# Turning a graph's adjacency as packed bytes on VectorE instead of as bf16 on TensorE

## The chip, the cores and the metric

The kernel runs on one core of a Trainium2 chip. The metric is the device time of one execution in microseconds (us), lower is better. Engines are named as in the profile: PE is TensorE (PEld its weight loads), DVE is VectorE, ACT is ScalarE, POOL is GpSimd, SP is SyncE, which here only issues DMAs. Each engine works through its own instructions in order; between engines they wait for each other by semaphores.

## The reference

64 graphs of 256 nodes with 512 features go through two pre-norm attention layers whose attention is masked by the graph's adjacency. Layer 0 has 4 heads of 64, layer 1 has 8. Cut to what matters:

```python
h = relu(layernorm(x))
q, k, v = heads(h @ Wq), heads(h @ Wk), heads(h @ Wv)
sim = einsum('bhid,bhjd->bhij', q, k) * scale
sim = where(adjacency_mask[:, None], sim, -max)      # layer 1: graph_mask | eye, else -1e9
x = x + einsum('bhij,bhjd->bhid', softmax(sim), v) @ Wo + bo
```

`adj` comes as one byte per entry (0 or 1), 256 x 256 for each graph. In layer 0 a row without any neighbour becomes a uniform softmax; layer 1 always has the diagonal.

## The kernel before

**Steps.** Two graphs make one step, so there are 32 steps (`NSTEP`), and T = 512 tokens in a step, kept as four tiles of 128 rows. Three steps are in work at once: while layer 1 of step s runs, layer 0 of step s+1 is finished and layer 0 of step s+2 is begun. One such period takes 95.67 us in the middle of the run.

**Order.** Nothing is scheduled automatically on PE, DVE, ACT and POOL. `at(period, place, fn, ...)` writes an event with a place; the events are sorted by place and the instructions of each engine stand in that order. A period is 6.4 places long. Within it PE has: 0.0 to 1.0 the first q and k of layer 1 (line 817); 1.0 the output combination of layer 1 of the step before (line 914, 28 instructions, seen as 56 records); 2.0 a visit (weighing by probabilities, line 1041, then new scores, line 970) and the values of layer 1 (line 898); 3.0 the combination of layer 0 of step s+1 (line 914, 14 instructions, 28 records); 3.5 the second q and k of layer 1 (817); 4.5 a visit and q, k of layer 0 of step s+2 (817); 5.5 the values of layer 0 (864); 6.2 a third visit.

**Products.** Every large matrix product is done as 7 block products (Winograd's scheme), numbered 1 to 7. Each fills a PSUM bank, and an "evacuation" (`evacuate`, `accumulate`, lines 746 to 785) takes the bank out and adds it into its place, on DVE for most products and on ACT for products 1 and 2. There are four banks in rotation (`mm_tile`), and a bank can be written again only when its evacuation is done. Three products go into a bank that another has used, on top of what stands in it (`SHARED = {2: 1, 4: 7, 3: 5}`): product 4 is accumulated in product 7's bank, so it may start only after product 7 has been evacuated. The tuples `SET`, `SETC` and `SETC0` are the orders in which the seven are done; `SETC0` is that of layer 0's combination, (1, 6, 5, 2, 7, 3, 4). After some products POOL adds a common term `u` to a block of `xt` (line 785).

**The adjacency.** The scores are computed with the keys on the partitions, so the adjacency has to be turned. For a step: `load_adjacency` (line 488) brings the bytes by SP's queue at place 1.0 of the period before; `adjacency_cast` (513, POOL, place 0.45) makes bf16 of them; `adjacency_turn` (563, place 2.5, in the midst of layer 1's values) turns eight 128 x 128 blocks on PE into a bank, and ACT copies the bank to `adT` (568). `mask0` (574, 577, POOL, place 3.1) makes layer 0's mask (adT - 1) * 1e30 and multiplies it by the row's "has neighbours" flag `ne`; `mask1` (582, 585, place 5.85) makes layer 1's. `adb` and `adT` share one buffer (tag "ab"). `neighbours` (521, DVE) reduces the bytes to the flags.

**Other work near it.** On DVE the sums over keys are turned and reduced (`turn_keys`, `key_quarters`, lines 1011 and 1018; `turn_sums`, `key_sums`, lines 1071 to 1083); DVE also turns h in 32 x 32 blocks (`turn_blocks`, 700), which SP moves by DMA (712). On POOL stand the sums of the probabilities' halves (`key_halves`, 1005), the division by the sums (`normalise`, 1116), the block sums for the products (`act_sums0`, `act_sums1`, 405 to 410) and the biases (`first_bias` 508, `second_bias` 652). `first_bias` for the four token tiles, in the order 2, 3, 0, 1, is at places 2.34, 2.5, 2.85, 2.86.

Of the kernel before, what the change touches and what calls it, by code (L numbers as in the profile page):

```python
# [8 lines left out]
FP = mybir.dt.float32  # L9
BF = mybir.dt.bfloat16  # L10
U8 = mybir.dt.uint8
I32 = mybir.dt.int32
AF = mybir.ActivationFunctionType
ALU = mybir.AluOpType

EPS = 1e-5
BIG = 1e30
# [298 lines left out]
def fast_path(  # L316
# [19 lines left out]
    nc = tc.nc  # L336
    P = 128
    B, N, D = x.shape
    DH = 64
    G = 2  # L340
    NSTEP = B // G
    NIC = N // P
    NT = G * NIC
# [9 lines left out]
    act = ctx.enter_context(tc.tile_pool(name="act", bufs=1))  # L353
# [10 lines left out]
    def mm_tile(shape, dt=FP, hold=False):  # L364
        tag = next(b for b in banks if b not in held)
        banks.remove(tag)
        banks.append(tag)
        if hold:
            held.add(tag)
        return ps_mm.tile(shape, dt, name="mm", tag=tag)  # L370

    identb = const.tile([P, P], BF, name="identb")
# [16 lines left out]

    NB = 7
    A_OF = {(0, 0): 0, (0, 1): 1, (1, 0): 2, (1, 1): 3}
    B_OF = ((0, 6, 5), (1, 3, 1))
    PRODUCT = {1: (0, 0), 2: (1, 1), 3: (6, 2), 4: (3, 6), 5: (2, 3), 6: (4, 4), 7: (5, 5)}
# [78 lines left out]
    S = [dict() for _ in range(NSTEP)]  # L474
# [10 lines left out]

    def load_adjacency(s):
        ad = S[s]["ad"] = io.tile([P, NT, N], U8, name="ad", bufs=1)
        nc.sync.dma_start(ad, adj[s * G:(s + 1) * G].rearrange("g (t p) j -> p (g t) j", p=P))

    def load_x(s):  # L490
        if s < NSTEP - 1:
# [16 lines left out]
        nc.gpsimd.tensor_tensor(xt[:, t, :], xt[:, t, :], bo_b, ALU.add)  # L508


    def adjacency_cast(s):
        S[s]["adb"] = act.tile([P, NT, N], BF, name="adb", tag="ab")
        nc.gpsimd.tensor_copy(S[s]["adb"], S[s]["ad"])

    def neighbours(s, g):

# [37 lines left out]
        ne = S[s]["ne"] = act.tile([P, T], FP, name="ne")  # L554
        nc.scalar.copy(ne, pn)

    def adjacency_turn(s):
        adb = S[s]["adb"]
        pa = mm_tile([P, NIC, G, N], BF)
        for g in range(G):  # L560
            for kc in range(NIC):
                for ic in range(NIC):
                    nc.tensor.transpose(  # L563
                        pa[:, kc, g, ic * P:(ic + 1) * P],
                        adb[:, g * NIC + ic, kc * P:(kc + 1) * P], identb,
                    )
        S[s]["adT"] = act.tile([P, NIC, G, N], BF, name="adT", tag="ab")
        nc.scalar.copy(S[s]["adT"], pa)

    def mask0(s):  # L570

        st = S[s]
        n0 = st["n0"] = act.tile([P, NIC, G, N], BF, name="n0")
        nc.gpsimd.tensor_scalar(n0, st["adT"], -1.0, BIG, op0=ALU.add, op1=ALU.mult)
        for kc in range(NIC):
            v = n0[:, kc].rearrange("p g n -> p (g n)")
            nc.gpsimd.tensor_tensor(v, v, st["ne"], ALU.mult)

    def mask1(s):
        st = S[s]  # L580
        n1 = st["n1"] = act.tile([P, NIC, G, N], BF, name="n1", bufs=2)
        nc.gpsimd.tensor_scalar(n1, st["adT"], -1.0, BIG, op0=ALU.add, op1=ALU.mult)
        for kc in range(NIC):
            v = n1[:, kc, :, kc * P:(kc + 1) * P]
            nc.gpsimd.tensor_tensor(v, v, offdiag, ALU.mult)
# [104 lines left out]

        return s == 0 or s == (1, NSTEP - 1)[lyr]

    Q, NQ = 32, P // 32

    def turn_blocks(s, lyr, t):

# [409 lines left out]
    def inverse_place(s, lyr, pr, i):  # L1106

        if (s, lyr) != (NSTEP - 1, 1):
            return S[s]["invb"][i]
        if pr == 0:  # L1110
            return wqk0[:, 6].rearrange("p c k o -> p (c k o)").rearrange("p (g n) -> p g n", g=G)
        return act.tile([P, G, N], FP, name="invb", tag=("n0", "ne", "ab")[pr - 1])

    def normalise(s, lyr, pr):
        dst, invb = S[s].pop(("dst", lyr, pr)), S[s].pop(("invb", lyr, pr))
# [10 lines left out]
    def at(period, place, fn, *args):  # L1126
        events.append((period * (PERIOD if period >= 0 else FIRST) + place, len(events), fn, args))
# [10 lines left out]

    SET = (1, 6, 5, 2, 7, 3, 4)
    SETC = (1, 5, 2, 6, 7, 3, 4)  # L1140
    SETC0 = (1, 6, 5, 2, 7, 3, 4)

    def visit(period, w, prev, cur):

# [51 lines left out]
    AT_X, AT_C0, AT_QK, AT_Q0, AT_V0, AT_H1, AT_Z = 2.0, 3.0, 3.5, 4.5, 5.5, 6.06, 6.2  # L1196
# [8 lines left out]
    p = NSTEP - 2  # L1205
# [9 lines left out]
    FIRST_C0, FIRST_Q0, FIRST_V0, FIRST_H1 = 3.0, 3.64, 4.64, 5.2  # L1215
# [5 lines left out]
    for s in range(NSTEP):  # L1221

        p = s - 2
        if s == 1:
            p -= 3.93 / FIRST
        at(p - 1 if s != 1 else -2, 3.2 if s == 1 else 5.7 if s < 3 else AT_H1 + 0.01, load_h, s)
        at(p - 1 if s != 1 else -2, 3.2 if s == 1 else 5.7 if s < 3 else 1.0, load_adjacency, s)
        at(p, (2.0, 2.4)[s] if s < 2 else 0.45, adjacency_cast, s)
        for t in range(NT):
            at(p, (0.5 + 0.4 * t, 1.95 + 0.1395 * t)[s] if s < 2 else (0.95, 1.05, 1.2, 1.35)[t], norm0, s, t)  # L1230
            if s == 0:
# [15 lines left out]
        else:  # L1247
            at(p, 2.3 if s == 2 else 0.05, neighbours_line, s)
            at(p, 2.31 if s == 2 else 0.051, neighbours_spread, s)
        at(p, (FIRST_Q0 + 0.1425, 3.583)[s] if s < 2 else 2.5, adjacency_turn, s)  # L1250
        at(p, (FIRST_Q0 + 0.3, 3.74)[s] if s < 2 else 3.1, mask0, s)
        at(p, (FIRST_Q0 + 0.31, 4.43)[s] if s < 2 else 5.85, mask1, s)
        if s == 0:
# [11 lines left out]
        if s < 2:  # L1265
            for t in range(NT):
                place = (FIRST_V0 + 0.14 * t - (0 if t else 0.0005), (4.31, 5.02, 5.16, 5.31)[t])[s]
# [7 lines left out]
        p = s - 1  # L1275
        if s == 0:
            p -= 2.23 / FIRST
        edge = 0 if s == 0 else 1 if s == NSTEP - 1 else 2
# [3 lines left out]
            at(p, AT_X - 0.000145 if s > 1 else 1.2, load_graph, s, 1)  # L1282
            at(p, AT_X + 0.0051 if s > 1 else 1.2, load_graph, s, 0)
        for k, t in enumerate(NORM1):
            at(p, (1.55, 1.5, (2.34, 2.5, 2.85, 2.86)[k])[edge], first_bias, s, t)
        if edge == 2:
            at(p, 2.8, lambda s=s: act_sums0(S[s]["oT0"]))
            at(p, 2.81, lambda s=s: act_sums1(S[s]["oT0"]))
# [7 lines left out]
        for k in range(NT):  # L1296
# [6 lines left out]
            place = ((3.6112, 3.6113, 3.7502, 3.7503)[k], 3.6 + 0.01 * k, AT_Q0 + (-0.0002, -0.00019, 0.0002, 0.00021)[k])[edge]  # L1303
# [11 lines left out]
        p = s  # L1315
        if s < NSTEP - 1:
# [3 lines left out]
            p, place = (s + 1, 1.0) if s < NSTEP - 2 else (s, LAST_QK + 2)  # L1320
# [96 lines left out]
```

## Time and profile before

| what | us |
|---|---|
| median of 3 runs (lowest, highest) | 3114.69 (3114.12, 3115.24) |
| the profiled execution | 3115.69 |
| its span, first to last instruction | 3113.6 |
| PE busy in the span | 3091.8 (99%) |
| DVE, POOL, ACT busy | 2453.8, 2242.3, 1235.3 |

The profile's page gives the busy time of each engine, the chain of work that ended last (followed back from the end, at each step to what released it), and groups of equal instructions with the mean duration of one. The timeline gives instructions in order of time; a number in brackets is the idle time of the engine before, with what ended it. Matmuls are pipelined, so the duration of one record is longer than its share of PE; what one costs is the distance from its start to the next one's start. The granted TensorE clock is full in this execution (1.00).

### The profile page before, as it was taken

What the parts mean: (1) busy time and instruction counts of PE and PEld (TensorE: products, weight loads), DVE (VectorE), ACT (ScalarE), POOL (GpSimd) and SP (SyncE); (2) the same over time, 40 slices, a digit from 0 to 9 for tenths busy, and PEclk for the clock granted to TensorE, in tenths of its full rate; (3) what the DMA queues carried; (4) which work ended last, traced back from release to release, by engine and by line L of the source; (5) the groups of instructions that cost most, each with busy time, mean ns of one, the idle gap of its engine ahead of it and who ended that gap; (6) DMA issues with size and microseconds to landing.
All of it is one profiled execution on the core that took longest, in us unless ns stands there. A gap on an engine that the chain in (4) does not pass through costs nothing.

```text
span 3113.6 us, 55568 instructions
## 1 busy us (share of the span) xinstructions
PE 3091.8 (99%) x20362; PEld 2538.7 (82%) x20362; DVE 2453.8 (79%) x4371; ACT 1235.3 (40%) x2166; POOL 2242.3 (72%) x2128
## 2 busy tenths in 40 slices
PE   8999999999999999999999999999999999999998
PEld 6888888888888888888888888888888888888787
DVE  6877877878877788787788777887777878778766
ACT  4434343344434343443434334443434344343431
POOL 7877776777767767767777677776776776777753
PEclk9999999999999999999999999999999999999999
DMA  4233232332322322223313233222232222331311
GB/s 138 64 98 92 55 91 72 92 93 67 83 71 87 93 87 66 84 72 99 93 53 93 72 91 93 73 79 77 80 93 86 67 82 74 99 93 51 91 34 49
DMA packets 187589, 251.22 MB, mean 81 GB/s; under 512 B 58088, under 2 KB 78192, under 8 KB 187312
## 3 DMA queue, kind: packets, MB, share of 16 engines
q1 hardware_dynamic: 139088, 183.74, 21.0%
q10 hardware_dynamic: 48224, 63.87, 7.0%
q8 instruction: 164, 2.69, 0.4%
q14 instruction: 113, 0.93, 0.1%
HBM read 128.59 MB, written 34.34 MB: 52 GB/s over the span
## 4 chain that ended last, share of the span: by engine, by line
PE 94%; POOL 3%; DMA 1%; DVE 1%; issue 1%; SPq 0%; ACT 0%; ACTq 0%; POOLq 0%; DVEq 0%
PE mm L817 37%; PE mm L914 17%; PE mm L898 11%; PE sc L970 8%; PE mm L864 6%; PE sc L1041 6%; PE mm L1041 5%; PE mm L970 2%; POOL pd L1005 1%; POOL xt L508 1%; PE mm L847 1%; DMA h<-blocks 0%; PE mm L940 0%; DMA out_dram<-xt 0%; PE mm L563 0%
## 5 line engine op out<-in xcount | busy, mean ns | idle before, releaser
L817 PE MATMUL mm<-hT,wqkv 128*128 128x256 f32 x3584 | 788.3, 380 | 0.6 <-DVE qk L757 0.6
L817 PEld LDWEIGHTS mm<-hT,wqkv 128*128 128x128 f32 x3584 | 677.6, 190 | 103.2 <-issue 11.4
L1005 POOL TENSOR_TENSOR pd<-p 128x512 f32<-128x512 f32 x383 | 479.4, 1273 | 337.9 <-ACT p L998 196.2
L914 PE MATMUL mm<-wo,oT 128*128 128x256 f32 x2632 | 586.1, 380 | 4.2 <-DVE xt L774 2.4
L914 PEld LDWEIGHTS mm<-wo,oT 128*128 128x128 f32 x2632 | 497.3, 190 | 83.2 <-issue 9.2
L998 ACT ACTIVATE p<-p 128x512 f32<-128x512 f32 x766 | 440.8, 626 | 118.2 <-DVE p L993 106.2
L993 DVE TENSOR_TENSOR p<-sc,n 128x512 f32<-128x512 f32 x579 | 363.0, 683 | 145.1 <-PE sc L970 145.1
L898 PE MATMUL mm<-wqkv,hT 128*128 128x256 f32 x1792 | 402.1, 382 | 0.4 <-ACT v L751 0.4
L817 PE MATMUL mm<-hT,wqk 128*128 128x256 f32 x1792 | 398.7, 382 | 0.3 <-ACT qk L751 0.2
L817 PEld LDWEIGHTS mm<-hT,wqk 128*128 128x128 f32 x1792 | 338.3, 191 | 55.9 <-issue 10.3
L898 PEld LDWEIGHTS mm<-wqkv,hT 128*128 128x128 f32 x1792 | 335.5, 190 | 54.2 <-issue 10.3
L970 PE MATMUL sc<-qk 64*128 64x256 f32 x2320 | 294.0, 385 | 1.7 <-DVE p L993 1.7
L785 POOL TENSOR_TENSOR xt<-xt,u 128x512 f32<-128x512 f32 x183 | 231.2, 1272 | 78.2 <-DVE xt L774 37.1
L970 PEld LDWEIGHTS sc<-qk 64*128 64x128 f32 x2320 | 218.1, 186 | 62.8 <-issue 27.9
L1011 DVE STREAM_TRANSPOSE turned_p<-pd 128x1024 f32<-128x1024 f32 x192 | 237.1, 1235 | 29.5 <-POOL pd L1005 29.5
L606 ACT ACTIVATE h<-h,mr,r 128x512 f32<-128x512 f32 x252 | 187.6, 803 | 169.6 <-POOL mr L602 169.6
L1116 POOL TENSOR_TENSOR oT<-oT 128x512 f32<-128x512 f32 x188 | 240.0, 1277 | 2.2 <-DMA oT<-line 2.2
L1018 DVE TENSOR_REDUCE part<-turned_p 128x32 f32<-128x1024 f32 x192 | 233.2, 1215 | 4.4
L1041 PE MATMUL sc<-p,v 128*32 128x256 f32 x3152 | 190.8, 382 | 0.0
L864 PE MATMUL mm<-hT,wv 128*128 128x256 f32 x840 | 188.6, 382 | 0.0
L864 PEld LDWEIGHTS mm<-hT,wv 128*128 128x128 f32 x840 | 156.5, 190 | 27.2 <-ACT vT L751 6.2
L1041 PE MATMUL mm<-p,v 128*32 128x256 f32 x2976 | 177.6, 379 | 0.0
(153 smaller groups left out, 4219.2 us busy)
## 6 DMA issues: line engine op xcount, KB each, us to landing
h<-blocks SPq DMA_DIRECT2D x960, 64.0 KB, 2.0
oT<-line SPq DMA_DIRECT2D x376, 128.0 KB, 3.1
h<-in_x_dram SPq DMA_DIRECT2D x31, 1024.0 KB, 8.7
xt<-in_x_dram ACTq DMA_DIRECT2D x60, 512.0 KB, 4.3
out_dram<-xt SPq DMA_DIRECT2D x31, 512.0 KB, 3.1
out_dram<-xt ACTq DMA_DIRECT2D x31, 512.0 KB, 4.5
v<-values ACTq DMA_DIRECT2D x480, 32.0 KB, 1.9
ne<-ne SPq DMA_DIRECT2D x90, 64.0 KB, 2.0
```

The source lines that it names most:

```text
L817: nc.tensor.matmul(bank[:, k, :], w[:, wa, c, k, a * P:(a + 1) * P], st["hT"][:, ba, c, :], start=first and (k, c) == (0, 0), stop=(k, c) ...
L864: nc.tensor.matmul(bank, wv0[:, wa, c, :], st["hT"][:, ba, c, :], start=first and c == 0, stop=c == HC - 1, skip_group_check=True,)
L898: nc.tensor.matmul(bank[:, t, :], st["hT"][:, ba, c, t * P:(t + 1) * P], wqkv1[:, wa, c, 2, :], start=first and (t, c) == (0, 0), stop=(t, ...
L914: nc.tensor.matmul(bank[:, t, :], oT[:, ba, c, t * P:(t + 1) * P], w[:, wa, c, :], start=first and (t, c) == (0, 0), stop=(t, c) == (NIC - ...
L970: nc.tensor.matmul(sc[g][e][:, kc, :], qk[rows, 1, k0:k0 + P], qk[rows, 0, g * N:(g + 1) * N], start=True, stop=True,)
L993: nc.vector.tensor_tensor(p[e][:, g], sc[e], neg[:, :, g, :], ALU.add)
L998: nc.scalar.activation(p[e][:, g], p[e][:, g], AF.Exp, scale=SCALE)
L1005: nc.gpsimd.tensor_tensor(st["pd"][:, e], p[e][:, :, 0, :], p[e][:, :, 1, :], ALU.add)
L1011: nc.vector.transpose(st["turned_p"], st.pop("pd").rearrange("p e g (b k) -> p (e g b) k", k=32))
L1018: nc.vector.tensor_reduce(st["part", lyr, prs][:, i], st.pop("turned_p"), axis=mybir.AxisListType.X, op=ALU.add)
L1041: nc.tensor.matmul(po[r0:r0 + 32, g, :], (st["v1"][:, g * NIC + kc, pr * P + r0:pr * P + r0 + Q] if lyr else st["v0"][:, r0 // Q, pr, g * ...
L1116: nc.gpsimd.tensor_tensor(dst, dst, invb, ALU.mult)
```

## The change

From step 2 on the adjacency stays in bytes. `adjacency_pack` (POOL) adds 64 to each byte and stores it so that the four bytes of one place in the step's four row tiles lie side by side and form one 32-bit word. `adjacency_turn` (DVE) turns these words in 32 x 32 blocks: 16 instructions, in four groups `a` of four, each from the 32 partitions of `a` to the 32 partitions of `b`. The mask is made from the turned bytes by POOL with a step of four bytes (`mask`: (byte - 65) * 1e30). The eight PE turns and ACT's copy of these steps are gone; steps 0 and 1 keep them.

The pack of a step stands one period earlier than the cast did, at place 4.9 (step 2: 0.45). The four groups of turns stand at places 1.571, 1.714, 1.857 (behind three evacuations of layer 1's combination) and at 1.99969 (behind the four line 700 instructions of that place, ahead of the visit's score masks). `load_adjacency` from step 3 on is issued by ACT's queue, at place 1.3. Three of the four `first_bias` move to 2.85, 2.86, 2.87. `SETC0` becomes (1, 6, 5, 7, 2, 3, 4). One buffer `both` (2 KB in each partition, as "ab" had) holds the packed and the turned words.

```diff
+    Q, NQ = 32, P // 32
     NB = 7
+    MARK = 64.0
...
     def load_adjacency(s):
         ad = S[s]["ad"] = io.tile([P, NT, N], U8, name="ad", bufs=1)
-        nc.sync.dma_start(ad, adj[s * G:(s + 1) * G].rearrange("g (t p) j -> p (g t) j", p=P))
+        (nc.sync if s < 3 else nc.scalar).dma_start(ad, adj[s * G:(s + 1) * G].rearrange("g (t p) j -> p (g t) j", p=P))
...
+    both = act.tile([P, 2, NIC, P, NT], U8, name="both")
+    flat = both.rearrange("p h k j t -> p (h k j t)")
+
     def adjacency_cast(s):
-        S[s]["adb"] = act.tile([P, NT, N], BF, name="adb", tag="ab")
-        nc.gpsimd.tensor_copy(S[s]["adb"], S[s]["ad"])
+        nc.gpsimd.tensor_copy(flat.bitcast(BF), S[s]["ad"].rearrange("p t n -> p (t n)"))
+
+    def adjacency_transpose(s):
+        adb = flat.bitcast(BF).rearrange("p (t n) -> p t n", t=NT)
+        pa = mm_tile([P, NIC, G, N], BF)
...
+        nc.scalar.copy(flat.bitcast(BF), pa.rearrange("p k g n -> p (k g n)"))
+
+    def adjacency_pack(s):
+        nc.gpsimd.tensor_scalar(
+            both[:, 0].rearrange("p k j t -> p t k j"), S[s]["ad"].rearrange("p t (k j) -> p t k j", j=P),
+            MARK, None, op0=ALU.add,
+        )
+
+    def adjacency_turn(s, a):
+        words = flat.bitcast(FP).rearrange("p (h k j) -> p h k j", h=2, k=NIC)
+        for b in range(NQ):
+            nc.vector.transpose(
+                words[b * Q:(b + 1) * Q, 1, :, a * Q:(a + 1) * Q], words[a * Q:(a + 1) * Q, 0, :, b * Q:(b + 1) * Q]
+            )
+
+    def mask(s, n):
+        if s < 2:
+            edges, one = flat.bitcast(BF).rearrange("p (k c i) -> p k c i", k=NIC, i=P), 1.0
+        else:
+            edges, one = both[:, 1].rearrange("p k i t -> p k t i"), 1.0 + MARK
+        nc.gpsimd.tensor_scalar(
+            n.rearrange("p k g (c i) -> p k (g c) i", i=P), edges, -one, BIG, op0=ALU.add, op1=ALU.mult
+        )
...
-    def adjacency_turn(s):
-        adb = S[s]["adb"]
-        pa = mm_tile([P, NIC, G, N], BF)
...
-        S[s]["adT"] = act.tile([P, NIC, G, N], BF, name="adT", tag="ab")
-        nc.scalar.copy(S[s]["adT"], pa)
...
-        nc.gpsimd.tensor_scalar(n0, st["adT"], -1.0, BIG, op0=ALU.add, op1=ALU.mult)
+        mask(s, n0)
...
-        nc.gpsimd.tensor_scalar(n1, st["adT"], -1.0, BIG, op0=ALU.add, op1=ALU.mult)
+        mask(s, n1)
...
-    SETC0 = (1, 6, 5, 2, 7, 3, 4)
+    SETC0 = (1, 6, 5, 7, 2, 3, 4)
...
-        at(p - 1 if s != 1 else -2, 3.2 if s == 1 else 5.7 if s < 3 else 1.0, load_adjacency, s)
-        at(p, (2.0, 2.4)[s] if s < 2 else 0.45, adjacency_cast, s)
+        at(p - 1 if s != 1 else -2, 3.2 if s == 1 else 5.7 if s < 3 else 1.3, load_adjacency, s)
+        if s < 2:
+            at(p, (2.0, 2.4)[s], adjacency_cast, s)
+            at(p, (FIRST_Q0 + 0.1425, 3.583)[s], adjacency_transpose, s)
+        else:
+            at(*((p, 0.45) if s == 2 else (p - 1, 4.9)), adjacency_pack, s)
...
-        at(p, (FIRST_Q0 + 0.1425, 3.583)[s] if s < 2 else 2.5, adjacency_turn, s)
+        for a in range(NQ if s > 1 else 0):
+            place = (2.05, 2.2, 2.86, 2.9)[a] if s == 2 else AT_X - 0.00031 if a > 2 else 1 + (a + 4) / 7 - 0.0005
+            at(p, place, adjacency_turn, s, a)
...
-            at(p, (1.55, 1.5, (2.34, 2.5, 2.85, 2.86)[k])[edge], first_bias, s, t)
+            at(p, (1.55, 1.5, (2.34, 2.85, 2.86, 2.87)[k])[edge], first_bias, s, t)
```

## The prediction

> **What bounds the kernel now.** I read the page first: busy shares, then the chain.
>
> ```profile
> PE 3091.8 (99%) x20362; PEld 2538.7 (82%) x20362; DVE 2453.8 (79%) x4371; ACT 1235.3 (40%) x2166; POOL 2242.3 (72%) x2128
> PE 94%; POOL 3%; DMA 1%; DVE 1%; issue 1%; SPq 0%; ACT 0%; ACTq 0%; POOLq 0%; DVEq 0%
> ```
>
> PE is never idle for long and the chain is 94% PE, so a change pays what it takes off PE or what PE no longer waits. Then I took one period (95.67 us, like its neighbours) and read PE's timeline, and the chain in order of time for the same stretch.
>
> ```profile
> 1553.63 0.61 PE L563 MATMUL mm<-identb,adb 128*128 128x128 bf16 x8
> 1554.08 5.40 PE L898 MATMUL mm<-wqkv,hT 128*128 128x256 f32 x24
> 1559.31 6.46 PE L914 MATMUL mm<-wo,oT 128*128 128x256 f32 x28
> 1565.61 12.25 PE L817 MATMUL mm<-hT,wqkv 128*128 128x256 f32 x56
> ...
> 1559.48 5.18 PE mm L914 x24
> 1564.66 0.01 issue
> 1564.67 1.10 PE mm L914 x4
> ```
>
> The reader sees two things PE could be spared. The eight turns lie between values products. And layer 0's combination is cut after 24 of 28 records: product 4, the seventh, starts late. DVE's timeline says why, and also shows where DVE has room:
>
> ```profile
> 1563.03 0.69 DVE L776 TENSOR_TENSOR xt<-mm,xt 128x512 f32<-128x512 f32 x1 [0.17 <-PE mm L914]
> 1563.83 0.69 DVE L774 TENSOR_TENSOR xt<-mm,xt 128x512 f32<-128x512 f32 x1
> ...
> 1536.03 0.69 DVE L774 TENSOR_TENSOR xt<-mm,xt 128x512 f32<-128x512 f32 x1 [1.04 <-PE mm L914]
> ...
> 1539.48 0.69 DVE L779 TENSOR_TENSOR xt<-mm,xt 128x512 f32<-128x512 f32 x1 [1.03 <-PE mm L914]
> 1540.09 2.48 DVE L700 STREAM_TRANSPOSE blocks<-h 128x512 f32<-128x512 f32 x4
> 1544.13 1.29 DVE L993 TENSOR_TENSOR p<-sc,n 128x512 f32<-128x512 f32 x2 [1.56 <-PE sc L970]
> ```
>
> Product 7's evacuation (second line 774, 1563.83) ends at 1564.52, and product 4, which goes into product 7's bank, starts at 1564.67.
>
> **Part 1, the turns leave PE.** In a values stage without turns a record takes 0.216 us (24 in 5.18, the chain's line above). From the first turn to the combination's start pass 1559.31 - 1553.63 = 5.68; the 24 records between need 5.18. The turns with the hand-over back to f32 therefore cost 0.50 us of PE a step, in 30 steps (2 to 31): 15.1 us. All of it is on the path, since PE is busy before and behind.
>
> **Part 2, products 7 and 2 swap.** The combination takes 1565.61 - 1559.31 = 6.30; 28 records at 0.216 are 6.05. So 0.25 us a step go to the wait for product 7's bank, in each period of the middle; 30 combinations (steps 1 to 30): 7.5 us. With 7 fourth instead of fifth, its evacuation moves ahead of line 776. Combination starting 0.50 earlier (1558.81): product 7 is done at 1562.27, evacuated by about 1563.15, product 4 wants the bank at 1558.81 + 24 x 0.216 = 1563.99. The wait is gone with 0.7 us to spare. What is late next there: product 3 into product 5's bank, evacuated by 1562.3 and wanted at 1563.13; product 7's own new bank, that of the last values product, evacuated about 1559.7 (line 763) and wanted at 1561.4. Neither binds. The rest of the bank rotation shifts by one place, because one user of a bank is gone, and I find no pair closer than these.
>
> **Part 3, DVE's 16 turns.** The nearest row is the 32 x 64 turn of line 1071, the same size and also with a change of partitions:
>
> ```profile
> L1071 DVE STREAM_TRANSPOSE keys<-part 32x64 f32<-32x64 f32 x380 | 87.5, 230 | 3.9
> L530 DVE STREAM_TRANSPOSE ne<-any_of 32x128 f32<-32x128 f32 x120 | 35.7, 298 | 1.2
> ```
>
> In the timeline four of line 1071 start from 1565.30 and the next work starts at 1566.30: 0.25 us each, so a group is 1.0 us, a step 4.0, the run 120 us of DVE (79% to 83%). Three groups lie in the holes of 1.03 to 1.04 us (ahead of lines 774 and 779, and of 781 between them), the fourth in the 1.56 us ahead of line 993. I take the cost on the path as nothing. If the cover fails: behind a group waits the evacuation of product 7, 3 or 4 of layer 1's combination. Product 4 wants product 7's bank at 1537.57, and evacuation 7 ended at 1536.72, so a group may overrun by 0.7 us. With line 530's 298 ns as the upper end, a group is 1.25 us, the overrun 0.2: still nothing. The lower end is also nothing.
>
> The Trainium skill ("VectorE: DVE Perf Modes", Rules for kernel authors) sends a 128 x 128 transpose to TensorE where PSUM will do as the destination, and keeps VectorE's for 32 x 32 blocks; it speaks against this part. Rival (d) is what that would be here; the rows show holes on DVE and none on PE, and the rule knows nothing of either.
>
> **Part 4, POOL.** The cast (1.04 us) goes and the pack (byte in, byte out at a step of four) comes; both masks now read bytes at a step of four. No row shows such a step. Lower end: 1.04 to 1.05 us as now, since a contiguous byte input already runs like bf16 in the cast. Upper end: 2.3 us, the rate of line 577's two inputs (1164 ns for 512). I take 1.05, the row with one input and 1024 elements.
>
> ```profile
> 1562.80 1.05 POOL L574 TENSOR_SCALAR n<-adT 128x1024 bf16<-128x1024 bf16 x1
> 1563.93 2.29 POOL L577 TENSOR_TENSOR n<-n,ne 128x512 bf16<-128x512 bf16 x2
> 1566.18 2.49 POOL L785 TENSOR_TENSOR xt<-xt,u 128x512 f32<-128x512 f32 x2
> ...
> 1592.63 2.50 POOL L1005 TENSOR_TENSOR pd<-p 128x512 f32<-128x512 f32 x2 [3.69 <-DVE turned_p L1011]
> ```
>
> The pack at 4.9 falls into the 3.69 us hole: nothing up to 3.6 us. The second mask (1604.45) has layer 1's block sums behind it; line 408's sum ends at 1609.47 and PE wants it at 1612.4: 2.9 us. The first mask is the tight one: POOL is busy from 1552.44 to 1568.67 without a hole. Behind it stand the two line 785 sums, which end at 1568.67; DVE's statistics (line 590) read them at 1569.94, about 1569.4 after the change. That is 0.7 us; then DVE is 0.5 us ahead of PE's next bank (in the line 817 stage product 7's evacuation, line 757, ends at 1575.19; product 4 wants the bank at 1565.61 + 48 x 0.216 = 1575.98; PE gains 0.75 on it and DVE 0.5). So the first mask may grow by 1.2 us before PE waits: at the upper end 0.05 us a step, 1.5 us in all.
>
> Moved in the queue: the three line 508 biases go behind the block sums, so these (405 to 410) come 1.23 us earlier and the last bias ends at 1562.7 as before; product 2, which needs it, is now evacuated later. In one period (2326.48) a late xt load made PE wait 0.77 us for line 408 and then 0.65 at the bank; both should shrink, 1 us in all. Where the cast stood (1618.93) POOL comes 1.0 us earlier to the sums ahead of layer 1's combination, which PE does not wait for.
>
> **Part 5, ACT and the queues.** The copy (1.01 us a step) goes; ACT is 40% busy: nothing. The load of the bytes moves to ACT's queue, one issue of about 0.39 us in a hole of 5.9 us ahead of the line 606 scalings. On SP it waited 3.9 us for the cast, with line 1089 behind it, which itself waits until 1626.08: no gain there. The pack reads the bytes 3.6 places (some 44 us) after the issue, landing takes 2.4.
>
> **Sum**, against the profiled execution's 3115.69: 15.1 + 7.5 + 1 = 23.6, giving 3092.1. The median lies 1.0 below that execution: 3091.
>
> **Rivals.**
> (a) The turns' gain comes, but PE meets another wait in layer 1's values or layer 0's combination, so the swap brings nothing. For it: from 1565.61 to 1577.79 DVE is busy 11.81 of 12.18 us and can't follow PE by more than 0.5. Against: the spare times above. 3114.7 - 15.1 = 3099.6.
> (b) Nothing net: both gains come back as waits, because DVE, with 120 us more, or POOL, full in front of the first mask, sets the pace of that stretch. Against: DVE's holes of 1 us and more in the same period. About 3114.
> (c) Slower: a byte step of four makes POOL element-bound. The first mask decides. Up to 2.25 us it is hidden; each us beyond is 30 us of the run; at 1.05 + 1.2 + 0.75 = 3.0 us the whole gain is eaten. At 4.2 us (four times the row) the run is 3091 + 30 x 1.95 = 3150. For it: no row has the step. Against: the cast's byte input costs nothing extra, and 4.2 lies beyond even two inputs.
> (d) Slower: the turns lie on the path. Their place is ahead of product 7's evacuation in layer 1's combination, and it decides from 0.43 us a turn (1.04 + 0.7 for four). With all 4.0 us of a step exposed the run is 3091 + 120 = 3211. For it: the holes are 0.04 us longer than a group. Against: 230 ns at the same size.
> The Trainium skill ("GPSIMD Engine Reference", Performance pitfalls for Q7 kernels) puts a surcharge of half on reads whose step is over 8 bytes; four bytes lie below. No run here shows it; by it the mask stays at 1.05, and with the surcharge about 1.6, hidden too.
>
> **How the numbers follow.** Forecast 0.65, (a) 0.17, (b) 0.06, (c) 0.10, (d) 0.02. The forecast's own range is 3088 (the last waits of late loads go too) to 3095 (the upper ends of parts 3 and 4 and a part of the swap lost). The range for 8 in 10 takes (a) in: 3087 to 3102. A measurement of this kernel tells about 0.2%, 6 us, from no change. Faster: forecast and (a), 0.82; same: (b), 0.06; slower: (c) and (d), 0.12.
>
> **What would show it.** In PE's timeline: 56 values records in one piece with no line 563 between them, and the combination 6.05 us long with no break before its last four. In the groups: the turn at 225 to 245 ns x480; pack and mask at 1.0 to 1.2 us. On DVE: no evacuation of layer 1's combination more than 0.2 us later behind PE than now. The prediction is wrong if a mask takes over 2.3 us, if the turn takes over 0.4 us, or if PE shows a new break of 0.2 us or more in each period.

## The result, and the profile after

| | us |
|---|---|
| before, median (lowest, highest) | 3113.62 (3111.23, 3115.24) |
| after, median (lowest, highest) | 3096.14 (3094.57, 3096.67) |
| after / before | 0.9943, 95% interval 0.9930 to 0.9956 |
| profiled executions, before and after | 3115.69 and 3096.28 |
| their spans | 3113.6 and 3094.5 |

The changed kernel is faster by 17.5 us in the medians and by 19.4 in the profiled executions, where the prediction had 23.6. The median lies in the range of 3087 to 3102, and 1.1 us above the narrower range of the forecast itself, 3088 to 3095. Line numbers of the changed kernel are 24 higher in most places: 817, 898, 914 and 970 are now 841, 922, 938 and 994.

The page of after, busy shares and chain:

```profile
PE 3072.8 (99%) x20122; PEld 2528.8 (82%) x20122; DVE 2555.7 (83%) x4851; ACT 1207.2 (39%) x2136; POOL 2301.9 (74%) x2128
PE 93%; POOL 3%; DVE 3%; DMA 1%; issue 1%; ACT 0%; SPq 0%; ACTq 0%; DVEq 0%; POOLq 0%
```

PE lost 240 instructions and 19.0 us of busy time, DVE gained 480 instructions and 101.9 us. PE still is the bound. PE's timeline of after, the stretch that answers to the one shown of before:

```profile
1542.07 12.35 PE L922 MATMUL mm<-wqkv,hT 128*128 128x256 f32 x56
1554.27 6.21 PE L938 MATMUL mm<-wo,oT 128*128 128x256 f32 x28
1560.31 12.25 PE L841 MATMUL mm<-hT,wqkv 128*128 128x256 f32 x56
```

The values are one piece of 56 records, and the combination has its 28 in one piece, 1560.31 - 1554.27 = 6.04 us from start to next start, where it was 6.30. Both gains are there in full. DVE's timeline of after, around the turns:

```profile
1530.37 0.97 DVE L540 STREAM_TRANSPOSE both<-both 32x64 f32<-32x64 f32 x4
1531.48 0.69 DVE L798 TENSOR_TENSOR xt<-mm,xt 128x512 f32<-128x512 f32 x1
1532.20 0.98 DVE L540 STREAM_TRANSPOSE both<-both 32x64 f32<-32x64 f32 x4
1533.22 0.69 DVE L805 TENSOR_TENSOR xt<-mm,xt 128x512 f32<-128x512 f32 x1
1533.94 0.98 DVE L540 STREAM_TRANSPOSE both<-both 32x64 f32<-32x64 f32 x4
1534.95 0.69 DVE L803 TENSOR_TENSOR xt<-mm,xt 128x512 f32<-128x512 f32 x1
...
1538.07 0.99 DVE L540 STREAM_TRANSPOSE both<-both 32x64 f32<-32x64 f32 x4
1539.59 2.48 DVE L1017 TENSOR_TENSOR p<-sc,n 128x512 f32<-128x512 f32 x4 [0.52 <-PE sc L994]
```

The four groups stand in the four holes. The evacuations behind them start 1.73 to 1.74 us apart, as before (1.73), and 0.52 us of the fourth hole is left. The groups of equal instructions in after (count, then busy us and mean ns of one):

```profile
L540 DVE STREAM_TRANSPOSE both<-both 32x64 f32<-32x64 f32 x480 | 112.9, 235 | 7.7
L532 POOL TENSOR_SCALAR both<-ad 128x1024 uint8<-128x1024 uint8 x30 | 92.4, 3080 | 0.0
L549 POOL TENSOR_SCALAR n<-both 128x1024 bf16<-128x1024 uint8 x60 | 62.6, 1043 | 4.5
```

The turn and the mask are as forecast. The pack takes 3.08 us, three times the value taken and above the upper end of 2.3. POOL's timeline of after shows why that costs nothing in the middle of the run:

```profile
1488.68 3.09 POOL L532 TENSOR_SCALAR both<-ad 128x1024 uint8<-128x1024 uint8 x1
1492.42 2.49 POOL L1029 TENSOR_TENSOR pd<-p 128x512 f32<-128x512 f32 x2 [0.65 <-DVE turned_p L1035]
```

It lies in the hole that was 3.69 us, and 0.65 are left.

**Where the missing 4 us went.** The start of a period is taken as the first record of layer 1's values in PE's timeline (line 898, now 922). Lengths of the periods in us:

| | first start | periods 0 to 4 | sixth start | periods 5 to 29 |
|---|---|---|---|---|
| before | 109.40 | 96.52, 96.16, 95.84, 95.67, 96.03 | 589.62 | 95.67; four longer: 95.95, 97.34, 95.76, 97.29 |
| after | 109.54 | 100.81, 95.72, 95.42, 94.92, 96.20 | 592.61 | 94.92, once 95.20 |

The steady period fell by 0.75, exactly the two terms (0.50 and 0.25). From the sixth start on the run is 22.1 us shorter: 25 x 0.75 = 18.75, and 3.4 by longer periods of before that are gone. Nearly all of the 3.4 are the periods of 97.34 and 97.29. The first is the one with the late load at 2326.48 in the prediction; in the second PE has the same two waits, 0.71 us for line 408 and 0.65 at the bank. But the sixth start itself comes 3.0 us later, where five periods should have made it 3.75 earlier. PE's timeline of after in that stretch:

```profile
107.88 1.73 PE L994 MATMUL sc<-qk 64*128 64x256 f32 x8 [1.30 <-DVE p L1017]
109.54 8.90 PE L922 MATMUL mm<-wqkv,hT 128*128 128x256 f32 x40
119.04 3.69 PE L922 MATMUL mm<-wqkv,hT 128*128 128x256 f32 x16 [0.60 <-DVE v L779]
122.57 2.75 PE L938 MATMUL mm<-wo,oT 128*128 128x256 f32 x12
126.48 1.97 PE L938 MATMUL mm<-wo,oT 128*128 128x256 f32 x8 [1.16 <-DVE v L787]
128.71 1.99 PE L938 MATMUL mm<-wo,oT 128*128 128x256 f32 x8 [0.26 <-DVE xt L798]
...
186.39 1.99 PE L841 MATMUL mm<-hT,wqkv 128*128 128x256 f32 x8 [0.75 <-DVE qk L779]
189.12 1.97 PE L841 MATMUL mm<-hT,wqkv 128*128 128x256 f32 x8 [0.74 <-DVE qk L781]
```

PE waits at seven places of this stretch (one, 0.21 us at 165.12, is left out above), mostly for DVE. Before had two of them:

```profile
107.75 1.73 PE L970 MATMUL sc<-qk 64*128 64x256 f32 x8 [0.77 <-DVE p L993]
...
184.70 1.97 PE L817 MATMUL mm<-hT,wqkv 128*128 128x256 f32 x8 [0.61 <-DVE qk L757]
```

Here the 16 turns of step 2 stand at places of their own (2.05, 2.2, 2.86, 2.9), and the pack of step 3 stands where POOL still sums weights. DVE's and POOL's timelines of after:

```profile
111.93 1.97 DVE L540 STREAM_TRANSPOSE both<-both 32x64 f32<-32x64 f32 x8
...
123.62 1.99 DVE L540 STREAM_TRANSPOSE both<-both 32x64 f32<-32x64 f32 x8
```

```profile
157.81 3.08 POOL L532 TENSOR_SCALAR both<-ad 128x1024 uint8<-128x1024 uint8 x1
```

None of these has idle time ahead of it, and the chain of after, in order of time, passes through turns of both DVE groups and through this pack.

### The profile page after: what moved, and what is told of

The parts are those of the page before. It is cut to its first block, busy times and chain, and to the rows that moved or that the text cites. A ratio compares the mean times of both kernels' runs of the same rounds, so it can differ in the third digit from the quotient of the medians.

```text
span 3094.5 us, 55510 instructions
## 1 busy us (share of the span) xinstructions
PE 3072.8 (99%) x20122; PEld 2528.8 (82%) x20122; DVE 2555.7 (83%) x4851; ACT 1207.2 (39%) x2136; POOL 2301.9 (74%) x2128
## 4 chain that ended last, share of the span: by engine, by line
PE 93%; POOL 3%; DVE 3%; DMA 1%; issue 1%; ACT 0%; SPq 0%; ACTq 0%; DVEq 0%; POOLq 0%
PE mm L841 36%; PE mm L938 17%; PE mm L922 11%; PE sc L994 8%; PE mm L888 6%; PE sc L1065 6%; PE mm L1065 5%; PE mm L994 2%; POOL pd L1029 1%; PE mm L871 1%; DMA h<-blocks 0%; PE mm L964 0%; DVE bs L615 0%; DMA out_dram<-xt 0%; POOL xt L809 0%
## 5 line engine op out<-in xcount | busy, mean ns | idle before, releaser
L938 PE MATMUL mm<-wo,oT 128*128 128x256 f32 x2632 | 579.1, 379 | 1.4 <-DVE v L787 1.2
L794 ACT COPY u<-mm 128x512 f32<-128x512 f32 x62 | 36.3, 585 | 369.9 <-PE mm L938 218.5
```

What stands on the lines that cost most here:

```text
L938: nc.tensor.matmul(bank[:, t, :], oT[:, ba, c, t * P:(t + 1) * P], w[:, wa, c, :], start=first and (t, c) == (0, 0), stop=(t, c) == (NIC - ...
```

## The experiments

The runs were made in four sets, each beside the kernel before on the same chip (medians of before: 3115.88, 3113.75, 3113.94, 3113.94); ratios are to the before of the set. Times of different sets can differ by some 2 us for that reason alone.

### The two gains, one at a time

The kernel before with the new order alone:

```diff
-    SETC0 = (1, 6, 5, 2, 7, 3, 4)
+    SETC0 = (1, 6, 5, 7, 2, 3, 4)
```

> The kernel before with SETC0 = (1, 6, 5, 7, 2, 3, 4) and nothing else. Theory (the two parts add): the 0.25 us break ahead of product 4 goes in each period, the eight PE turns stay: period 95.67 -> 95.42, 30 combinations, 7.5 us, ratio about 0.9976. Rival (bank rotation): with the turns' bank still in the rotation, product 7 as fourth finds its new bank late and the break only moves ahead of product 7: period stays 95.67, ratio 1.000.

Measured 3104.38 (3104.05 to 3105.03), ratio 0.9964 (0.9951 to 0.9978). The steady period is 95.42, 0.25 below before. The mechanism and the size of part 2 are shown: 7.5 of the 11.5 us. Of the rest the two traces show 1.9 in the longer periods of before, which became shorter, and 0.9 in an earlier first start. That start differs between 108.2 and 110.7 among the kernels here, with no order that was found.

The changed kernel with the old order:

```diff
-    SETC0 = (1, 6, 5, 7, 2, 3, 4)
+    SETC0 = (1, 6, 5, 2, 7, 3, 4)
```

> The changed kernel with SETC0 = (1, 6, 5, 2, 7, 3, 4) as before. Theory (the two parts add): 0.50 us a period from the turns, period 95.67 -> 95.17, 15.1 us less 5 us lost in the period in which step 2 is turned: about 3103.5, ratio 0.997. The break of 0.25 us ahead of product 4 stays. Rival (DVE paces this stretch): without the swap DVE, which starts the combination no earlier relative to its own work, keeps PE longer at the bank; the break grows to 0.5 us and more, period 95.4 or more, time 3109 or more.

Measured 3110.97 (3109.51 to 3116.25), ratio 0.9989 (0.9980 to 0.9998). The steady period is 95.18, 0.50 below before, as part 1 and the theory have it, while the time is the rival's. For stretches of 95.3 to 96.1 take 4.3 us of it back, and the first five periods, 486.3 us against 480.2 before, take more. DVE's and PE's timelines of this kernel in such a period:

```profile
2707.99 0.69 DVE L800 TENSOR_TENSOR xt<-mm,xt 128x512 f32<-128x512 f32 x1 [1.13 <-POOL xt L510]
2708.59 0.68 DVE L798 TENSOR_TENSOR xt<-mm,xt 128x512 f32<-128x512 f32 x1
```

```profile
2709.42 1.10 PE L938 MATMUL mm<-wo,oT 128*128 128x256 f32 x4 [0.76 <-DVE xt L798]
```

With the old order product 2 (line 800) stands ahead of product 7 (line 798) on DVE, and it needs a bias that POOL adds behind the block sums. DVE waited 19.4 us at line 800 for POOL's line 510 in this run, 4.4 in the changed kernel. So the swap is worth 13 to 15 us here (3107.7 against 3094.5 in the spans; 3110.97 against 3096.14 in the medians, which are of different sets): besides its 0.25 it takes product 7 out from behind the bias. The kernel before, with the old order and the biases at their old places, waited 5.6 us for the bias at this product (line 776 there). That the move of the bias is what makes the old order so sensitive fits these waits, but is not shown: a run of the old order in the changed kernel with the biases back was not made.

### The moves beside them

The changed kernel with the biases and the bytes' load undone together:

```diff
-        (nc.sync if s < 3 else nc.scalar).dma_start(ad, ...)
+        nc.sync.dma_start(ad, ...)
...
-        at(..., 5.7 if s < 3 else 1.3, load_adjacency, s)
+        at(..., 5.7 if s < 3 else 1.0, load_adjacency, s)
...
-            at(p, (1.55, 1.5, (2.34, 2.85, 2.86, 2.87)[k])[edge], first_bias, s, t)
+            at(p, (1.55, 1.5, (2.34, 2.5, 2.85, 2.86)[k])[edge], first_bias, s, t)
```

> The changed kernel with the four line 510 biases back at 2.34, 2.5, 2.85, 2.86 and the load of the bytes back on SP's queue at place 1.0. Theory (these moves cost and bring nothing in a period without late loads): period 94.92 as in the changed kernel, time 3096 within 2 us; a late xt load may show a break of up to 0.8 us ahead of product 6 of layer 0's combination. Rival (the moves carry part of the gain): the block sums, 1.23 us later while PE comes 0.5 us earlier, make PE wait in each period: over 0.1 us a period, 3099 or more.

Measured 3115.43 (3112.79 to 3117.29), ratio 0.9999 (0.9990 to 1.0008): the whole gain is gone. That is a plain miss of parts 4 and 5, which gave these moves 1 us. The two edits were then made one at a time. The load alone (the first two pairs of lines above):

> The changed kernel with one edit: the adjacency bytes of steps 3 and on are loaded by SP's queue again (place 1.0) instead of ACT's. On SP the load stands right behind the pack that frees its buffer, directly ahead of the 16 transfers of line 736 that bring layer 1's h. With this load on SP and the biases back the run was 3115.4. Theory L (the load did that): on SP the load waits for the pack's end (3.08 us long), the 16 transfers start some 1.2 us later than in the changed kernel, and where they take more than their usual 10.03 us to issue (10.6 to 11.6 in periods of the second half) ACT's scaling of line 749 and PE's scores of line 994 come late: periods of 95.5 to 96.7 in the second half, 3108 to 3116 in all. Theory B (the biases did it): as the changed kernel, 3095 to 3097, periods 94.92 throughout.

Measured 3111.28 (3109.40 to 3113.97), ratio 0.9993 (0.9984 to 1.0003). The biases alone (the last pair):

> The changed kernel with one edit: the biases of line 510 back at places 2.34, 2.5, 2.85 and 2.86, so that one of them stands ahead of the block sums on POOL as before. The prediction called this move worth 1 us in all. Theory L (the load's queue is what cost 19 us with both moves undone): 3096 to 3099, periods of 94.92 with a late one here or there. Theory B (the biases did it): 3108 to 3116, with PE waiting ahead of layer 0's combination for the block sum of line 408 in many periods.

Measured 3097.04 (3096.91 to 3099.03), ratio 0.9950 (0.9933 to 0.9966), 0.9 above the changed kernel. That is within the spread of the runs, but the trace has 0.86 of it in four periods (0.09 to 0.35 each), at the start of layer 0's combination, where PE waits for a block sum of POOL (line 410): the size and the place that part 4 had. So it is the load. POOL's, SP's, ACT's and PE's timelines of the kernel with the load on SP, in a period of 96.90:

```profile
2638.85 3.08 POOL L532 TENSOR_SCALAR both<-ad 128x1024 uint8<-128x1024 uint8 x1
```

```profile
2641.96 0.40 SPq L490 DMA_DIRECT2D ad<-in_adj_dram  x1
2642.53 10.26 SPq L736 DMA_DIRECT2D h<-blocks  x16
```

```profile
2656.09 2.93 ACT L749 ACTIVATE hT<-h,gb 128x512 f32<-128x512 f32 x4 [4.84 <-DMA h<-blocks]
2658.93 0.56 ACT L1080 COPY oT<-sc 128x512 f32<-128x512 f32 x1
```

```profile
2659.54 0.91 PE L994 MATMUL sc<-qk 64*128 64x256 f32 x5 [1.03 <-ACT oT L1080]
```

And of the changed kernel, POOL's and SP's of the same step:

```profile
2627.71 3.08 POOL L532 TENSOR_SCALAR both<-ad 128x1024 uint8<-128x1024 uint8 x1
```

```profile
2629.64 10.04 SPq L736 DMA_DIRECT2D h<-blocks  x16
```

On SP the load stands directly ahead of the 16 transfers that bring layer 1's h, and not where it stood before the change (there between lines 537 and 1089, with the 16 transfers some 19 us later). SP's order isn't set by `at`. It waits for the pack, which reads the buffer that it fills: the pack ends at 2641.93, the load is issued at 2641.96, the transfers begin at 2642.53. That is 3.68 us after the pack's start, against 1.93 with the load on ACT's queue. The groups say what the 1.75 us mean (line 749 in the changed kernel, then with the load on SP):

```profile
L749 ACT ACTIVATE hT<-h,gb 128x512 f32<-128x512 f32 x120 | 88.0, 803 | 68.5 <-PE mm L888 63.5 <-DMA h<-blocks 5.0
```

```profile
L749 ACT ACTIVATE hT<-h,gb 128x512 f32<-128x512 f32 x120 | 88.0, 804 | 102.0 <-DMA h<-blocks 86.4 <-PE sc L994 6.9 <-PE mm L888 4.5
```

ACT's scalings now wait for the transfers in nearly every period (26 times against 2). Where these land in their usual time PE does not notice (94.92). Where they take longer to issue (10.03 us at best; in the changed kernel 10.25 to 11.63 from 1490 to 2300 us) or to land, ACT's copy of line 1080 and with it PE's scores come late. Laid beside a steady period of the changed kernel, record by record, the longer periods from the sixth start on (by 0.2 to 2.0 us) lose nearly all of it at these scores, but for one period, 0.3 longer, that the changed kernel has too. Theory L holds. Undone together the two moves give a median 4.2 us above that of the load alone, but in another set; the ratios differ by 0.0006, which is within their intervals, so more than the sum of the two isn't shown.

### The start of the run

Step 2 left on the old way (cast, eight turns on PE, copy by ACT), and step 3's pack at place 0.45 of period 1:

```diff
     def mask(s, n):
-        if s < 2:
+        if s < 3:
...
-        if s < 2:
-            at(p, (2.0, 2.4)[s], adjacency_cast, s)
-            at(p, (FIRST_Q0 + 0.1425, 3.583)[s], adjacency_transpose, s)
+        if s < 3:
+            at(p, (2.0, 2.4, 0.45)[s], adjacency_cast, s)
+            at(p, (FIRST_Q0 + 0.1425, 3.583, 2.5)[s], adjacency_transpose, s)
...
-            at(*((p, 0.45) if s == 2 else (p - 1, 4.9)), adjacency_pack, s)
+            at(*((p, 0.45) if s == 3 else (p - 1, 4.9)), adjacency_pack, s)
...
-        for a in range(NQ if s > 1 else 0):
+        for a in range(NQ if s > 2 else 0):
```

> The changed kernel, but step 2 keeps the cast, the PE turns and ACT's copy (the pack of step 3 then stands at place 0.45 of its own period). Theory (what is missing against the forecast is step 2's start): the period in which step 2 is turned falls from 100.8 us to 95.9 to 96.5, nothing else changes but one period's 0.5 us: 3096.1 -> 3091.3 to 3092, ratio to before about 0.993. Rival (the loss of that period belongs to the moved biases, the swap or the first bytes loaded by ACT): the period stays near 100 us and the time at 3096.

Measured 3090.72 (3090.10 to 3091.67), ratio 0.9921 (0.9908 to 0.9935). The first period is 96.57, the sixth start 586.80 in place of 592.61. It is the fastest version here and beats both kernels. It changes two things at once, so three further runs take them apart. Without step 2's turns alone (its mask is then made from bytes that were not turned, and its factor is 1):

```diff
-            ..., edges, -one, BIG, op0=ALU.add, op1=ALU.mult
+            ..., edges, -one, BIG if s != 2 else 1.0, op0=ALU.add, op1=ALU.mult
...
-        for a in range(NQ if s > 1 else 0):
+        for a in range(NQ if s > 2 else 0):
```

> The changed kernel without the 16 turns on DVE of step 2 alone (step 2's mask is then made from bytes that were not turned, with the factor 1 in place of 1e30; turning and the strength of that one mask are left out). Step 2's pack on POOL, 3.08 us at place 0.45, stays. In the changed kernel the first period of the steady form takes 100.81 us against 96.52 before and 96.57 with all of step 2 on PE. Theory T (the turns cost it, since DVE has no holes there): that period falls to 96.6 to 97.5, the run to 3091.5 to 3093. Theory K (the pack costs it, by holding back POOL's sums of line 1029): 100 or more, 3095 to 3097. Shared: in between.

Measured 3094.74 (3093.51 to 3096.47), ratio 0.9934 (0.9918 to 0.9951). Neither theory as written: the first period falls by 1.6 only, the next two grow, and the sixth start is 592.45. PE's timeline of this kernel:

```profile
163.73 3.72 PE L888 MATMUL mm<-hT,wv 128*128 128x256 f32 x16 [1.28 <-ACT vT L775]
...
176.84 7.17 PE L841 MATMUL mm<-hT,wqkv 128*128 128x256 f32 x32 [0.22 <-POOL hT L410]
```

PE's waits for DVE ahead of the first combination are shorter or gone, but what PE gained it loses some 40 us later, where POOL is behind: the pack of step 3 (157.81 in the changed kernel, 3.08 us) stands in a row of POOL's work that has no hole from 144 to 183 us in this kernel too. So the next two runs move that pack:

```diff
-            at(*((p, 0.45) if s == 2 else (p - 1, 4.9)), adjacency_pack, s)
+            at(*((p, 0.45) if s < 4 else (p - 1, 4.9)), adjacency_pack, s)
```

> The changed kernel with one edit: step 3's pack (3.08 us on POOL) stands at place 0.45 of period 1 instead of 4.9 of period 0, where POOL has no hole (sums of weights stand there besides). In the changed kernel the sixth values stage starts at 592.6 us; without step 2's turns on DVE also at 592.5 (the first period 1.6 shorter, the next two 1.1 longer); with all of step 2 on PE and step 3's pack late at 586.8. Theory P (two causes side by side, step 2's turns on DVE and step 3's pack on POOL, and taking one away leaves the other to set the time): 591 to 593, the run 3094 to 3096. Theory Q (step 3's pack is the cause): 587 to 588, the run 3090 to 3091.5. Theory R (step 2's own pack at place 0.45 of period 0): 592.5, the run 3096.

Measured 3094.37 (3093.30 to 3095.12), ratio 0.9935 (0.9918 to 0.9951), sixth start 590.97. Both edits together:

> The changed kernel with both edits: no turns on DVE for step 2 (left out: the turning of that step, and its mask's factor is 1 in place of 1e30), and step 3's pack late as in the run beside it. Step 2's pack stays at place 0.45 of period 0. Theory P (two causes side by side): the sixth values stage starts at 587 to 588.5, the run at 3090 to 3092, while either edit alone gives little. Theory Q: as with step 3's pack late alone. Theory R (step 2's own pack): 592, 3095 to 3096.

Measured 3091.40 (3090.60 to 3092.29), ratio 0.9927 (0.9910 to 0.9943), sixth start 586.75. Taking the turns away gives 0.2 us at the sixth start, moving the pack 1.6, both 5.9. The first start, which no edit here was meant to move, differs between these runs (109.54 in the changed kernel, 108.62 with both edits), so the five periods alone say it better: they sum to 483.06 in the changed kernel, 482.87 without the turns, 481.06 with the pack moved, 478.13 with both and 477.81 with step 2 on PE. That is 0.2, 2.0, 4.9 and 5.3 us. Theory P holds: two causes side by side, DVE by step 2's turns and POOL by step 3's pack. The forecast would have had 476.5 (480.22 - 3.75); the 1.3 to 1.7 us that are left weren't followed. Step 2's own pack, which all three keep, costs next to nothing (3091.40 against 3090.72).

### The margins that the prediction named

Each turn issued twice from step 3 on:

```diff
-        for b in range(NQ):
+        for b in [b for b in range(NQ) for _ in range(2 if s > 2 else 1)]:
```

> The changed kernel with each of the 16 turns on DVE issued twice from step 3 on (same data): a group takes 2.0 us instead of 1.0, 4.0 us a step more on DVE, 116 us in the run. The prediction gave a group 0.7 us of overrun before PE waits; here it overruns its hole of 1.03 by about 0.97, so 0.27 us a step, 8 us: about 3104, periods 95.2. Rival (d), the turns on the path: 4.0 us a step, 3212. If DVE had room for all of it: 3096.

Measured 3263.35 (3260.06 to 3264.94), ratio 1.0481 (1.0463 to 1.0498): 167 us above the changed kernel where 8 were expected and rival (d) had 116. DVE's and PE's timelines of this kernel:

```profile
1611.92 2.06 DVE L540 STREAM_TRANSPOSE both<-both 32x64 f32<-32x64 f32 x8
1614.01 0.69 DVE L803 TENSOR_TENSOR xt<-mm,xt 128x512 f32<-128x512 f32 x1
1614.62 2.48 DVE L724 STREAM_TRANSPOSE blocks<-h 128x512 f32<-128x512 f32 x4
1617.13 2.08 DVE L540 STREAM_TRANSPOSE both<-both 32x64 f32<-32x64 f32 x8
1619.25 2.49 DVE L1017 TENSOR_TENSOR p<-sc,n 128x512 f32<-128x512 f32 x4
```

```profile
1620.00 1.72 PE L994 MATMUL sc<-qk 64*128 64x256 f32 x8 [2.43 <-DVE p L1017]
```

The expectation looked at one bank. Product 4's start is late by 0.35 us in this trace (layer 1's combination against the changed kernel's), near the 0.27 worked out. But no group gives its overrun back, since DVE has no idle time between them: three overruns of 1 us add up, the fourth group comes on top, and DVE's mask of the scores (line 1017) starts 4.54 us after PE's scores, against 1.17 in the changed kernel. There PE is idle for 2.43 us (2.80 between two starts, 2.6 more than a record takes) in every one of the 29 periods, and its next eight scores, which follow DVE's masks one by one, lose another 0.7 where the clock stays full. With the 0.35 that makes 3.6 us of the 5.7 that a period is longer on average, near the 4.0 that the doubled turns add on DVE. The other 2.1 are a slower clock of PE behind the pause; the last section has it.

The first mask's instruction issued three times from step 3 on:

```diff
-        mask(s, n0)
+        for _ in range(3 if s > 2 else 1):
+            mask(s, n0)
```

> The changed kernel with the first mask's tensor_scalar (1.04 us) issued three times from step 3 on (same data): 2.08 us a step more on POOL, ahead of the mask's product with the flags. The prediction gave the first mask 1.2 us of growth before PE waits, and 30 us of the run for each us beyond: 0.9 us x 29 = 26 us, 3122, periods 95.8. If POOL's row of work ahead of DVE's statistics sets nothing: 3096. If each us shows fully: 60 us, 3156.

Measured 3136.86 (3134.46 to 3138.31), ratio 1.0074 (1.0057 to 1.0091). POOL's, DVE's and PE's timelines of this kernel (its lines are one higher from 600 on):

```profile
1579.56 3.30 POOL L549 TENSOR_SCALAR n<-both 128x1024 bf16<-128x1024 uint8 x3
```

```profile
1587.70 0.69 DVE L616 BATCH_NORM_STATS2 bs<-xt 128x6 f32<-128x512 f32 x1 [1.66 <-POOL xt L810]
...
1592.30 0.66 DVE L782 TENSOR_TENSOR qk<-mm,qk 128x512 f32<-128x512 f32 x1
```

```profile
1593.02 1.99 PE L842 MATMUL mm<-hT,wqkv 128*128 128x256 f32 x8 [0.86 <-DVE qk L782]
```

This is the chain of the prediction: the mask, the sums behind it, DVE's statistics, product 7's evacuation, product 4 on PE. The steady period is 96.05, 1.13 longer, for 2.26 us more of mask: a margin of 1.1 us, where the prediction had 1.2. The run is 15 us slower than expected, because a period grew by 1.13 instead of 0.9, because the stretch up to the sixth start, where POOL is behind already, grew by 8.8 in all (1.1 of it ahead of the first start), and because several later periods are 0.1 to 0.8 above 96.05.

### What makes the pack slow

The pack writing its bytes one behind the other:

```diff
-            both[:, 0].rearrange("p k j t -> p t k j"), S[s]["ad"].rearrange("p t (k j) -> p t k j", j=P),
+            flat[:, :NT * N], S[s]["ad"].rearrange("p t n -> p (t n)"),
...
-            ..., edges, -one, BIG, op0=ALU.add, op1=ALU.mult
+            ..., edges, -one, BIG if s < 2 else 1.0, op0=ALU.add, op1=ALU.mult
```

> The changed kernel with the pack writing its 1024 bytes one behind the other instead of at a step of four, from a plain read (left out: the interleaving, so the turned words are not the adjacency, and the mask's factor from step 2 on is 1 in place of 1e30). Theory S (the step of the write makes the pack 3.08 us): 1.04 us. Theory O (byte output with byte input is slow by itself): 3.08 us. In either case the run stays at 3093 to 3097, since the steady period's pack lies in a hole of POOL; only step 2's pack could give back part of the first period.

Measured 3094.27 (3094.26 to 3094.28), ratio 0.9934 (0.9914 to 0.9954). The pack's group in this kernel:

```profile
L532 POOL TENSOR_SCALAR both<-ad 128x1024 uint8<-128x1024 uint8 x30 | 83.5, 2784 | 0.0
```

The step of the write is 0.30 of the 3.08 us. The other 2.78 remain with plain bytes in and plain bytes out. The cast, with byte input and bf16 output, took 1.04 in the kernel before. The mask, the same kind of instruction as the pack with byte input at a step of four and one operation more, takes 1.04 too: it is the byte output that costs. Theory O holds but for 0.3 us.

## Why the prediction was right, and where it was wrong

- **Part 1** (turns leave PE): right, and to the size. 0.50 us in each steady period, alone and in the change.
- **Part 2** (swap): right, 0.25 us alone and in the change, and no next wait took its place in the steady period. Rival (a) fell. The part missed that the swap and the move of the bias seem to belong together: with the old order DVE waits 19.4 us for the bias ahead of product 7, against 5.6 in the kernel before. That the move of the bias is the cause was not shown by a run of its own.
- **Part 3** (DVE's turns hidden): right in the middle of the run, 235 ns a turn, four groups in four holes. Wrong in size at the start. The sum counted both gains in all 30 steps and read the holes from one period of the middle. Step 2's 16 turns have other places, where DVE has no hole; the part never looked there. With step 3's pack, which part 4 put into "the 3.69 us hole" of that same period, this is the term that was left out: the sixth start was to come 3.75 us earlier and came 3.0 later, 6.7 us. Taken away together the two give back 4.9 in the five periods; 1.7 stays open, and the rest is the first start.
- The margin of 0.7 us behind a group was right for the one bank it was worked out for, and wrong as the point from which rival (d) decides: overruns add up over the groups, the scores behind the fourth wait longest, and of the 4.0 us a step that were added 3.6 then show, where the margin left 0.27. That is near rival (d)'s price; PE's clock comes on top, so that 167 us were measured, above the 120 that it named as the most. The Trainium skill ("VectorE: DVE Perf Modes", Rules for kernel authors), which sends this transpose to TensorE, was not borne out in the middle of the run, where PE had no room and DVE had; in the first period, where DVE had none, moving step 2 back to PE was part of the faster version.
- **Part 4** (POOL): the mask was right, 1.04 us, and so was the chain behind it (margin 1.1 for 1.2). The pack was mis-sized, 3.08 us for 1.05, because neither of the rows it was taken from writes bytes: line 574 has bf16 in and out, the cast bytes in and bf16 out. Its upper end, 2.3, was too low as well. That cost nothing in the steady period only because the hole was 3.69. The bias move was right in place and about in size, though 0.9 us for 1 is not clear of the noise of the medians.
- **Part 5** (ACT and the queues): "no gain there" was wrong. The load's place was read from the queue of before, where it waited for the cast at place 0.45. Once the pack frees the bytes earlier, the load on SP stands ahead of the 16 transfers of layer 1 and behind a 3.08 us pack. ACT's queue keeps some 13 to 15 us that would otherwise be lost (3107.6 against 3094.5 in the spans, 3111.28 against 3096.14 in the medians). The forecast time was not touched by this, since the changed kernel has the load on ACT, but the reason given for the term was.
- **The sum**: 23.6 forecast against 19.4 in the profiled executions. The start took 6.7, and longer periods of before that vanished gave 3.4 where 1 was counted, because before had two periods with those waits and not one: 23.6 - 6.7 + 2.4 = 19.3. So two errors of opposite sign bring the sum nearer, which is luck. The forecast of 3091 was 5 us low; the range held the time only by its wider bounds, which were set for rival (a), and (a) did not come. The version with step 2 on PE runs at 3090.7.
- Rivals (b) and (c): DVE and POOL set the pace only at the start. The step of four did not slow what binds: the reads cost nothing extra, as the Trainium skill ("GPSIMD Engine Reference", Performance pitfalls for Q7 kernels) has it for steps of up to 8 bytes, with 1043 ns here.

## What to carry to other kernels

A gain "per step" has to be checked in the first and last steps as well, where moved work has other places and the holes of the steady period don't exist; here that was 6 us of 24. When a buffer is freed earlier, ask where the transfer that fills it will then stand in its queue, what it waits for there, and what stands behind it. And when work is fitted into a row of holes, the margin isn't that of one hole: what overruns is carried on to the next until DVE is idle again.

## What the runs showed of the hardware

Byte output on POOL: a tensor_scalar over 128 x 1024 elements took 1.04 us with bytes in at a step of four and bf16 out (as long as the cast with bytes in at a step of one), 2.78 us with bytes in and out, and 3.08 us with the bytes written at a step of four.

PE's clock after a short pause: in the run with each turn issued twice PE was idle for 2.43 us in each of the 29 periods from step 3 on. In 26 of 29 periods some records after the pause were 427 ns apart in place of 216, 4 to 12 of them, and then full speed came back. The windows of that kernel show it (the last three numbers are the granted clock, the DMA share and GB/s):

```profile
1711.00:1718.00 7.00, 5.13 (x68) 3.41 (x60) 6.60 (x20) 1.17 (x2) 2.09 (x2) 1.00 0.74 243
1718.00:1724.00 6.00, 5.44 (x15) 4.06 (x16) 4.69 (x8) 2.36 (x4) 3.53 (x3) 0.55 0.70 202
1724.00:1730.00 6.00, 6.00 (x26) 5.19 (x25) 2.91 (x3) 2.67 (x5) 2.41 (x3) 0.88 0.50 129
```

The granted clock is 0.55 behind the pause and 0.88 in the next six us; the mean over the run was 0.978. Behind three of the 29 pauses the clock stays full; there the pause and the eight scores cost 3.3 us, and with product 4's 0.35 that is 3.6. So the clock's share of the 5.7 us is 2.1 on average.

The clock record of this trace tells more. Behind the pauses the clock is at half rate in 26 stretches of 3.41 or 6.83 us, 140 us in all and so 70 us of clock lost, some of it while PE was idle or waited for DVE anyway. All of them begin on one grid with steps of 3.41 us (213.28, 312.27, 414.67, ...). Where no such stretch followed, the pause lay across a border of this grid, with at most 1.77, 1.93 and 2.01 us of it on one side; the other 26 had 2.01 to 2.43 us on one side. So what counts here is how much of the pause falls into one piece of 3.41 us, and about 2.0 us was enough. The Trainium skill ("TensorE: Matmul & The Clock Gate", HAM oscillation) warns of idle gaps above some 3.4 us; here 2.43 us were enough, so the measurement narrows that rule. The pause lay behind the small products of the scores, and whether these count as less work was not tested. In the changed kernel no such pause exists in the steady period, and its granted clock is full from 16.5 to 3091.9 us.

The 16 block transfers of layer 1 are issued in 10.03 us at best and in up to 11.7; those of layer 0 take 10.6 to 15.1. Both were seen in every kernel here. What lengthens them in parts of the run wasn't settled.
